# Moving the weight corrections of the first macro to VectorE and two row statistics to ScalarE

## The chip, the core and the metric

The kernel runs on one core of a Trainium2 chip. The metric is the time on the device in microseconds (us), median over several executions. Five engines run side by side, each in its own order: TensorE (PE, with its weight loads as PEld), VectorE (DVE), ScalarE (ACT), GpSimd (POOL) and SyncE (SP), which here only issues DMAs. POOL issues the gathers. Everything is float32.

## The reference

The input x has 4096 rows of 1024 numbers. Cut to what matters:

```python
xn = layernorm(x)                                  # per row, eps 1e-5
corr = irfft(abs(rfft(xn))**2)                     # autocorrelation of a row
weights, delay = top_k(corr, 6)                    # 6 = int(log(1024))
s = sum_k softmax(weights)[k] * roll(xn, -delay[k])
def qlora(x, wq, A, B):                            # weights repeat 4 times along the input
    return x @ tile(wq, (1, 4)).T + 0.5 * x @ A.T @ B.T
g = silu(qlora(silu(qlora(xn, w1)) * qlora(xn, w3), w2))   # 1024 -> 2752 -> 1024
out = x + s * g
```

## The kernel before

**Tiles.** The rows are worked on in 8 macros of 512 rows (`NR`), each of 4 tiles `r` of 128 rows. For a macro, the object `Corr` makes the normalised rows, their folded and transposed forms (`yT`, `yU`, `cT`, `bT`) and the lags; the object `Ffn` makes the feed-forward part; `Gathers` sums the six rolled copies of each tile. The folding uses that the weights repeat: TensorE sees 256 folded inputs instead of 1024.

**Order.** Nothing is scheduled by a tool. The list of functions that `plan` returns puts work before (`pre`), within (`mid`, then `half`) and after (`end`) each of the 15 steps of a macro, and every engine runs its instructions in just that order. Steps 0 to 9 are `up`: step p works on part c = p // 2 of the hidden units, two of its four blocks j. Step 10 is the rest of the hidden units, and steps 11 to 14 are the product with w2. While macro m runs, the same steps also prepare macro m+1: `stats(r)` and `norm(r)` (mean, deviation, normalising, folding), `save(r)` (two copies to DRAM for the gathers), `turn(r)` (transposes on PE), and so on.

**One block of `up`.** PE adds four matmuls into two PSUM banks that ScalarE has seeded (`seed`, L546), for the gate and the up product. ScalarE takes Silu of the gate (L582) into z, then seeds the banks of the block two further on. VectorE multiplies z by the other bank (L584), and GpSimd adds z to the sum `zf`. PE's small matmuls `u` (L552) for the LoRA part of w2 read the four z of a part one block later. There are 5 banks for the seeded sums (`psf`), and 2 for everything else of PE (`ps`), the correlation sums `e` and `o` (L433) among them.

**The first macro** does more than the others. The seed and the LoRA terms take the place of one row of the weights, so this row, held in `w0`, has to be taken off all weights first: `lessen_part(c)` loads nothing itself, but runs two instructions for part c. L146 on VectorE corrects half k = 0 and L147 on GpSimd half k = 1, each 128x1024 (part 5: 128x384). `load_first(c)` issues the load of `w0` on SP. The corrected weights stay for all macros. Parts 0 and 1 are done ahead of the first step. Parts 2 to 5 are done at `end[1]`, `end[3]`, `end[5]` and `end[7]`. PE reads part c first at step 2c: part 2 in step 4, part 3 in step 6.

The tiles `w0_2` to `w0_5` are in the pool `p3` under the tag `s`, which has three buffers. The gathered sums `s_0_0`, `s_0_1`, `s_0_2` of the tiles are in the same three buffers after them: `s_0_0` lies where `w0_3` was. Its first instruction, on ScalarE (L513), is issued at the end of step 4, between the seeds of block gu_2_3 and the Silu of z_2_2.

Also in the first macro: `mix_weights` (four sums of halves of w2 on VectorE, L170 to L173, for a product with fewer matmuls), `power(g)` for the spectra (`squares`, with the tile `o2` on ScalarE and the sum on GpSimd), `join`, and the search for the lags of the macro's own tiles: `lags(r)` in `mid[2+r]` (`corr_r`, VectorE, and a mirrored copy of it by ScalarE, L451) and `search(r)` in `end[2+r]` (L458 to L468, the six highest values).

Names as used below: z_c_j is the z of part c, block j; gu_c_j_0 and gu_c_j_1 its two banks; corr_r, search_r, norm(r) belong to tile r; x_1_r is tile r of macro 1.

## Time and profile before

| | |
|---|---|
| Median of 3 runs | 1112.71 us (1111.41 to 1113.75) |
| The profiled execution | 1112.99 us, its span 1111.2 us |
| PE busy | 1086.4 us, 98% of the span |
| DVE busy | 781.5 us, 70% |
| ACT busy | 584.9 us, 53% |
| POOL busy | 680.3 us, 61% |
| Mean granted clock of PE | 0.994 |

A span runs from the first to the last instruction, and the small difference to the execution's time lies around it. A line of the page gives an engine's operation by its source line (L577), its tiles, its busy time, the mean of one, and the idle time before it with what ended that. "PEclk" is the share of TensorE's clock that was granted. The times of a timeline are us from the span's start. A line of a timeline holds a duration that includes what the instruction waited for after its issue, so the same operation can show 0.68 in one place and 2.83 in another.

### The profile page before, as it was taken

To read this page: it belongs to the slowest core of one execution; us is meant where nothing else is said; L and a number is where in the kernel's file an instruction comes from. 1 tells how busy PE (TensorE), PEld (TensorE's weight loads), DVE (VectorE), ACT (ScalarE), POOL (GpSimd) and SP (SyncE) were. 2 spreads that over 40 slices of the span, in tenths; PEclk is the share of its full clock that TensorE was granted. 3 is DMA by queue.
4 is the path that set the end of the run, shared out by engine and by line. 5 is a ranking of instruction groups with operands and counts; after the bars stand their busy time and mean duration, and the time that the engine had idled before them with its cause. 6 is when DMAs were issued, how large, how long until landed. Compare 5 with 4: busy or idle time off the path is not lost.

```text
span 1111.2 us, 10958 instructions
## 1 busy us (share of the span) xinstructions
PE 1086.4 (98%) x3350; PEld 467.5 (42%) x3350; DVE 781.5 (70%) x1218; ACT 584.9 (53%) x1049; POOL 680.3 (61%) x535
## 2 busy tenths in 40 slices
PE   5998999999999999999999999999999999999997
PEld 4344344443444434443344434444344443444432
DVE  6799888776677776777677767677767776664543
ACT  5646634675356653665436663376534675354531
POOL 3676866677347763667546773657735677356832
PEclk9998999999999999999999999999999999999999
DMA  9852566565365653566445664556536565253533
GB/s 368 367 214 76 195 203 218 198 209 181 97 213 198 206 168 118 193 218 193 140 153 180 207 199 133 170 195 211 183 104 199 199 208 173 84 188 119 162 99 123
DMA packets 65085, 201.70 MB, mean 182 GB/s; under 512 B 7514, under 2 KB 8026, under 8 KB 64132
## 3 DMA queue, kind: packets, MB, share of 16 engines
q0 software_dynamic: 27648, 100.68, 30.0%
q1 hardware_dynamic: 37380, 100.35, 25.0%
q8 instruction: 26, 0.43, 0.2%
q14 instruction: 31, 0.25, 0.1%
HBM read 150.61 MB, written 50.39 MB: 181 GB/s over the span
## 4 chain that ended last, share of the span: by engine, by line
PE 88%; DVE 5%; issue 3%; POOL 2%; DMA 1%; ACT 1%; SPq 0%; DVEq 0%; POOLq 0%
PE gu L577 47%; PE y L653 20%; PE gu L603 3%; PE u L552 3%; PE y L663 3%; PE t L238 2%; PE fe L386 1%; PE o L433 1%; PE e L433 1%; PE fe L389 1%; PE fo L386 1%; DMA x<-in_x 1%; PE ua L254 1%; PE fo L389 1%; PE u L560 1%
## 5 line engine op out<-in xcount | busy, mean ns | idle before, releaser
L577 PE MATMUL gu<-yT,w_sb 128*128 128x512 f32 x960 | 459.8, 600 | 1.0 <-ACT gu L546 1.0
L577 PEld LDWEIGHTS gu<-yT,w_sb 128*128 128x128 f32 x960 | 176.5, 191 | 234.6 <-issue 208.5
L494 POOL DMA_INDIRECT roll<-scr,lag x192 | 232.3, 1210 | 62.6 <-issue 29.0
L516 DVE SCALAR_TENSOR_TENSOR s<-roll,w,s 128x1024 f32<-128x1024 f32 x160 | 221.8, 1386 | 1.3 <-DMA roll<-scr,lag 0.4
L546 ACT ACTIVATE gu<-second,b_sb 128x512 f32<-128x512 f32 x320 | 208.2, 686 | 4.6 <-DVE z L584 3.5
L584 DVE TENSOR_TENSOR z<-z,gu 128x512 f32<-128x512 f32 x160 | 109.5, 684 | 111.1 <-PE gu L577 75.8
L589 POOL TENSOR_TENSOR zf<-zf,z 128x512 f32<-128x512 f32 x80 | 134.4, 1680 | 79.4 <-DVE z L584 77.9
L582 ACT ACTIVATE z<-gu 128x512 f32<-128x512 f32 x160 | 95.2, 595 | 140.0 <-PE gu L577 134.7
L577 PE MATMUL gu<-yU,w_sb 128*128 128x512 f32 x320 | 164.3, 595 | 0.0
L469 POOL TENSOR_TENSOR e<-euler,e 128x6 f32<-128x6 f32 x32 | 48.6, 1519 | 145.7 <-DVE e L468 144.4
L735 POOL TENSOR_TENSOR x<-g,x 128x512 f32<-128x512 f32 x62 | 82.3, 1336 | 66.1 <-DVE g L734 23.5
L653 PE MATMUL y<-w_sb,zf 128*128 128x512 f32 x256 | 122.1, 599 | 0.0
L577 PEld LDWEIGHTS gu<-yU,w_sb 128*128 128x128 f32 x320 | 61.0, 191 | 77.2 <-issue 67.5
L734 DVE TENSOR_TENSOR g<-s,g 128x512 f32<-128x512 f32 x64 | 52.7, 854 | 43.2 <-ACT g L733 42.4
L587 POOL TENSOR_TENSOR zf<-z,z 128x512 f32<-128x512 f32 x40 | 65.4, 1634 | 24.0 <-DVE z L584 17.6
L733 ACT ACTIVATE g<-y 128x512 f32<-128x512 f32 x64 | 35.5, 593 | 78.2 <-PE y L663 45.2
L653 PEld LDWEIGHTS y<-w_sb,zf 128*128 128x128 f32 x256 | 46.2, 190 | 59.8 <-issue 57.5
L451 ACT COPY corr<-corr 128x511 f32<-128x511 f32 x32 | 19.8, 617 | 80.6 <-DVE corr L450 80.6
L653 PE MATMUL y<-w_sb,S 128*128 128x512 f32 x128 | 61.8, 605 | 0.0
L653 PE MATMUL y<-t_sb,zf 128*128 128x512 f32 x128 | 60.4, 593 | 0.3 <-DVE zf L647 0.3
L214 DVE TENSOR_TENSOR a<-x 128x512 f32<-128x512 f32 x28 | 33.8, 1209 | 26.7 <-ACT x L207 26.7
L192 DVE BATCH_NORM_STATS2 stats<-x 128x6 f32<-128x512 f32 x64 | 40.8, 677 | 4.2 <-DMA x<-in_x 4.2
(179 smaller groups left out, 1371.4 us busy)
## 6 DMA issues: line engine op xcount, KB each, us to landing
scr<-x SPq DMA_DIRECT2D x64, 512.0 KB
x<-in_x SPq DMA_DIRECT2D x32, 512.0 KB
x<-in_x SPq DMA_DIRECT2D x64, 256.0 KB
out<-x SPq DMA_DIRECT2D x64, 256.0 KB
w_sb<-in_w13t SPq DMA_DIRECT2D x5, 1024.0 KB
second<-rows SPq DMA_DIRECT2D x14, 256.0 KB
roll<-scr,lag POOLq DMA_INDIRECT x192, 5.2
w<-in_w0t SPq DMA_DIRECT2D x5, 512.0 KB
```

The source lines that it names most:

```text
L469: nc.gpsimd.tensor_tensor(e, bass.AP(euler.tensor, euler.offset, [list(euler.ap[0]), [0, TOP]]), e, ALU.pow)
L494: nc.gpsimd.indirect_dma_start(out=g, out_offset=None, in_=st.scratch[r].rearrange("p (n o) -> (p n) o", o=1), in_offset=bass.IndirectOffs ...
L516: nc.vector.scalar_tensor_tensor(s, g, w, s, ALU.mult, ALU.add)
L546: nc.scalar.activation(acc, self.st.second[:, wi, :], AF.Copy, scale=b13_sb[:, c, q : q + 1])
L577: nc.tensor.matmul(acc, lhsT=w13_sb[:, c, 2 * j + wi, k, :], rhs=y, start=False, stop=(k == 1), skip_group_check=True,)
L582: nc.scalar.activation(z, accs[0], AF.Silu)
L584: nc.vector.tensor_tensor(z, z, accs[1], ALU.mult)
L587: nc.gpsimd.tensor_tensor(self.sum_of(c), zs[0], zs[1], ALU.add)
L589: nc.gpsimd.tensor_tensor(self.zf[c], self.zf[c], z, ALU.add)
L653: nc.tensor.matmul(acc, lhsT=lhs, rhs=rhs, start=(first and a == 0), stop=True, skip_group_check=True)
L734: nc.vector.tensor_tensor(g, s(i)[:, cols], g, ALU.mult)
L735: (nc.vector if last else nc.gpsimd).tensor_tensor(xt, g, xt, ALU.add)
```

## The change

Four edits, all of which bear on the first macro alone:

- `lessen` takes the engine of its second instruction. Parts 0 and 1 keep GpSimd; parts 2 to 5 now run both instructions on VectorE, at `end[2]`, `end[4]`, `end[6]` and `end[7]`.
- The statistics of tiles 2 and 3 of macro 1 are made by a new `stats_scalar`: a sum and two sums of squares on ScalarE, then three small instructions on GpSimd. Before, VectorE made them (L192 to L196) with two small ones on GpSimd.
- `power(3)` is put ahead of the last of the four sums of w2.
- `o2` of g = 1 and 3 in macro 0 goes to the buffer `bcs` of `p1`, where it was in `x2` of `px`.

```diff
-    def lessen(w, w0):
+    def lessen(w, w0, engine=nc.vector):
         nc.vector.scalar_tensor_tensor(w(0), w0, minus, w(0), ALU.mult, ALU.add)
-        nc.gpsimd.tensor_tensor(w(1), w(1), w0, ALU.subtract)
+        engine.tensor_tensor(w(1), w(1), w0, ALU.subtract)
...
+        def stats_scalar(self, r):
+            n, xt = f"{self.m}_{r}", self.x[r]
+            total, mean, var, rstd, shift = [
+                small.tile([P, 1], F32, tag=tag, name=f"{tag}{i}_{n}") for i, tag in enumerate(("rest", "var", "var", "rstd", "shift"))
+            ]
+            squares = small.tile([P, 2], F32, tag="mv", name=f"squares_{n}")
+            nc.scalar.activation(xt, xt, AF.Identity, accum_out=total)
+            nc.scalar.activation(mean, total, AF.Copy, scale=-1.0 / (32 * L))
+            for h in range(2):
+                left = p1.tile([P, 512], F32, tag="a", name=f"left_{n}_{h}")
+                nc.scalar.activation(
+                    left, xt[:, h * 512 : (h + 1) * 512], AF.Square, bias=mean, scale=1.0 / 32, accum_out=squares[:, h : h + 1]
+                )
+            nc.gpsimd.tensor_scalar(var, squares[:, 0:1], squares[:, 1:2], EPS, ALU.add, ALU.add)
+            nc.gpsimd.tensor_tensor(rstd, var, mhalf, ALU.pow)
+            nc.gpsimd.tensor_scalar(shift, mean, rstd, 32.0, ALU.mult, ALU.mult)
+            self.parts[r] = (shift, rstd)
...
-            o2 = (p1 if m else px).tile([P, NR], F32, tag="bcs" if m else "x2", name=f"o2_{m}_{g}")
+            where = (p1, "bcs") if m or g % 2 else (px, "x2")
+            o2 = where[0].tile([P, NR], F32, tag=where[1], name=f"o2_{m}_{g}")
...
-            mid[1].extend(mix_weights[2:])
-            mid[1].append(lambda: st.power(3))
+            mid[1].extend([mix_weights[2], lambda: st.power(3), mix_weights[3]])
...
-                end[2 * c - 3].append(lambda c=c: lessen_part(c))
+                end[(2, 4, 6, 7)[c - 2]].append(lambda c=c: lessen_part(c))
...
-                stats[r].append(lambda r=r: nxt.stats(r))
+                stats[r].append(lambda r=r: nxt.stats_scalar(r) if first and r >= 2 else nxt.stats(r))
...
-    def lessen_part(c):
+    def lessen_part(c, engine=nc.vector):
         w0 = first_times.pop(c)
         if c < FULL:
-            lessen(lambda k: w13_sb[:, c, :, k, :], w0)
+            lessen(lambda k: w13_sb[:, c, :, k, :], w0, engine)
...
-        lessen_part(0)
-        lessen_part(1)
+        lessen_part(0, nc.gpsimd)
+        lessen_part(1, nc.gpsimd)
```

## The prediction

> **What bounds the kernel now.** I read the page's busy shares first: PE is busy 98% of the span, so a change pays only where PE waits or runs slowly. Then I asked for PE's waits in the first 165 us. Over the whole span the list is the same, so all that can be won lies in the first macro:

> ```profile
> PE t L315 <- DVE b_first L290: 10.7, 2, 8.9
> PE e L433 <- DVE total L477: 1.8, 1, 1.8
> PE fo L389 <- ACT e L415: 1.2, 1, 1.2
> PE gu L577 <- ACT gu L546: 1.0, 1, 1.0
> PE u L552 <- DVE z L584: 0.6, 1, 0.6
> ```

> Columns: us in total, times, longest. The first is the program's start, which the change leaves alone. The next view cuts the span into stretches of 2 us (busy time of PE, PEld, DVE, ACT, POOL, then PE's granted clock, DMA share, GB/s):

> ```profile
> 84.00:86.00 2.00, 0.44 (x4) 0.24 (x3) 2.00 (x7) 0.00 (x0) 0.00 (x0) 1.00 0.00 0
> 86.00:88.00 2.00, 0.76 (x5) 0.60 (x5) 1.22 (x7) 1.83 (x4) 0.00 (x0) 0.81 0.00 0
> 90.00:92.00 2.00, 2.00 (x3) 0.80 (x3) 1.87 (x6) 1.52 (x4) 1.05 (x1) 0.50 0.00 0
> 94.00:96.00 2.00, 2.00 (x6) 0.96 (x5) 1.67 (x5) 0.71 (x2) 1.90 (x3) 0.98 0.79 242
> ```

> Two stalls close together (84.4 to 86.3 and 87.0 to 87.9) are followed by a clock of 0.50 from 87.3 to 94.0. PE worked from 87.9 on, so some 3.1 us are lost to the clock on top of 2.8 to the stalls. What made the stalls is in VectorE's and GpSimd's timelines:

> ```profile
> 57.88 2.83 DVE L214 TENSOR_TENSOR a<-x 128x512 f32<-128x512 f32 x1
> 69.07 0.69 DVE L214 TENSOR_TENSOR a<-x 128x512 f32<-128x512 f32 x1
> 77.74 2.30 DVE L146 SCALAR_TENSOR_TENSOR w_sb<-w,minus,w_sb 128x1024 f32<-128x1024 f32 x1
> 81.58 2.56 DVE L153 TENSOR_TENSOR yc<-a 128x256 f32<-128x256 f32 x1
> 99.43 1.28 DVE L146 SCALAR_TENSOR_TENSOR w_sb<-w,minus,w_sb 128x1024 f32<-128x1024 f32 x1
> ```

> ```profile
> 56.83 3.34 POOL L147 TENSOR_TENSOR w_sb<-w_sb,w 128x1024 f32<-128x1024 f32 x1
> 81.26 2.60 POOL L147 TENSOR_TENSOR w_sb<-w_sb,w 128x1024 f32<-128x1024 f32 x1
> ```

> L214 takes 0.69 alone and 2.83 beside L147: where both engines have an instruction with two SBUF operands, one waits until the other's has ended. L147 alone holds about 2.2 us (from 57.95, when L146 ended, to 60.17). The reader is to see that these waits made corr_2 late (86.1), and PE's matmul e with the seeds behind it.

> **The change, part by part.** The sum is made against the profiled execution's 1112.99 us (span 1111.2), 0.28 above the median.

> *Removed:* four L147 on POOL with their holds of 2.2 us; VectorE's statistics of two tiles, 1.6 each (63.97 to 65.60).

> *Added on VectorE:* four L147. The trace has none there. Bounds are 1.13 (L405, same size, start to start, alone) and 2.3 (L146 when it waited); I take 1.13, since POOL has little left that holds. L146 takes 1.19 start to start.

> *Added on ScalarE, twice:* a 1024-wide pass with a sum (1.13, and 0.22 to read it, as L207 shows), a scalar (0.20, L208), two 512-wide passes with sums (0.50 + 0.22 each), gaps: 3.1. Bounds: 2.1 (three passes alone) and 3.4 (full durations).

> *Added on POOL:* one small instruction, 0.3. POOL now waits for ScalarE's sums; behind that wait stands zf, which needs a later z in any case: 0. If it weren't so, 0.3 twice.

> *Sums of w2:* T4 (L173) steps behind bT_3, which can't start before ScalarE's o2 ends (50.55). VectorE idles 1.0 there and T4 ends at 53.0 for 51.8, but the join after it waited for POOL until 52.9 anyway: 0.1. *Buffers of o2:* PE's last reads of the tile in `bcs` ended before 21 us, 17 us earlier than o2 is written: 0; half a microsecond were a reader late. *SP:* the load of w0_5, and behind it that of x_1_3, waits for part 2: issued at 71 for 69.3. VectorE used x_1_3 at 92.8 without waiting; ScalarE wants it at 95: 0, and 2 if that slack were gone.

> Now the walk. Durations start to start, from the rows: search 2.87 (66.20 to 69.07), norm 2.6 (69.07 to 71.69), corr 0.8, z 0.6, s 1.2 on VectorE; Silu 0.5, a seed 0.62, the mirrored copy L451 0.55 on ScalarE.

> 1. norm(0) starts at 57.0, when POOL's zf ends, for 60.1. corr_0 ends at 60.9 for 64.05. But ScalarE now has the statistics of tile 2 ahead of the Silu of z_1_1: 60.95 + 0.55 + 3.1 = 64.6. That Silu ran at 64.61 before. VectorE's lead of 3 us is spent, and it idles 4 us.
> 2. z_1_1 starts at 65.2, search_0 ends at 68.7, part 2 at 71.0. PE wants its second half at 70.7: 0.3 lost.
> 3. norm(1), z_1_2 and corr_1 to 74.95 (before 73.05), copy and Silu, z_1_3 ends at 76.65. PE's u, which ended at 75.97, ends at 77.6: 1.65 lost so far.
> 4. search_1 to 79.5, norm(2) to 82.6 (0.5 for POOL's zf), corr_2 ends at 83.95 for 86.1. PE reaches e at 86.1 and finds corr_2 done, and the seeds too. The stalls of 1.84 and 0.95 and the slow clock are gone.
> 5. z_2_1 ends at 85.7, search_2 at 88.6, part 3 at 90.9. Here is a new wait: `s_0_0` lies where w0_3 was, so ScalarE's first gather instruction now waits for part 3's second half, which POOL had done at 83.9. Behind it on ScalarE stand the Silu of z_2_2 and the seeds of gu_3_0: 90.9 + 1.05 + 0.5 + 0.62 = 93.1. PE arrives at 89.95 and waits 3.1.
> 6. Second seed and oc_3 to 94.0, corr_3 to 94.8, copy 0.55, statistics of tile 3 3.1, Silu 0.5: z_2_3 ends at 99.65. PE's u for this z was due at 96.6 and ends at 100.6: another 3. Before, the transposes behind u began at 99.0. So PE, 1.4 ahead at gu_3_0, is behind: **+1.6**.
> 7. From z_2_3 on VectorE has s, search_3, z, s, weights, z, s, part 4 and norm(3) before the transposes of tile 3: 13.1, and 1.15 for one zf of POOL. PE needs 13.9 to get there: **+0.3**. Later PE waited for nothing before, and VectorE idles 1.4 and 2.0 between 115 and 120: 0.

> *Slow clock.* The waits of steps 5 and 6 can bring half clock too. Most would fall between them, where PE has 3 us to spare, so it is hidden; bounds 0 and 3.3. Taken: **+0.4**.

> [...]

> Sum: 1.6 + 0.3 + 0.4 = +2.3. From 1112.99, less the 0.28: **1115.0**.

> **Rivals.**

> *A, not slower: the statistics on ScalarE are short.* Both groups lie in the serial chain of steps 1 to 6. At the lower bound of 2.1, 2.0 of the 2.3 goes: 1113.0. Any group below 3.0 brings the sum under 0.2%. For it: passes overlap (L207 lasts 1.23 and starts the next after 1.13). Against: the reads and the scalar are in the rows.

> *B, faster: ScalarE isn't held by `s_0_0`*, because part 3 is done in time. Then z_2_2 follows part 3 at once, z_2_3 ends about 97.2, PE's u 98.15 for 99.0, without slow clock: 1112.2; together with A's 2.0, 1110.2. It decides if part 3 ends before 86. Against: it stands behind z_2_1 and search_2 in VectorE's order.

> *C, slower: the half clock isn't hidden*, or comes after step 6: 3.3 for my 0.4, 1117.9. For it: the one case in this trace cost all of its time. Against: PE waits for z_2_3 at either clock.

> *D, slower: GpSimd's `e` and gathers get between VectorE's instructions* of part 2 and norm(1), 0.94 a gather: up to 2 in step 2 and 1 in step 7: 1118. Against: at 99.43 `e` waited and L146 did not.

> **How the numbers follow.** About 0.2%, 2.2 us, is what a measurement tells from no change. The forecast, with sizes that give 1113.5 to 1116.5, gets 0.50: 0.30 slower by over 0.2%, 0.20 within. A 0.16 (within), B 0.12 (faster), C 0.12 and D 0.10 (slower). So faster 0.12, same 0.36, slower 0.52. The range leaves out most of B and the far ends of C and D: 1111.2 to 1118.6.

> **What would show it.** Right: no L214 or L153 of over 2 us at 57 and 81; no wait of PE's e there, and a clock of 1.00 from 84 to 89; ScalarE idle some 4.6 before the first `s`, released by VectorE's L147; PE's gu waiting for seeds, then u for z near 97. Wrong: if PE runs from 89 to 100 without a wait, step 5 or 6 is mistaken and B holds; if the transposes of tile 3 wait for over 1 us, step 7 was too small.

## The result, and the profile after

| | before | after |
|---|---|---|
| Median | 1111.63 us (22 runs, 1111.20 to 1113.88) | 1114.68 us (22 runs, 1114.30 to 1115.58) |
| The profiled execution | 1112.99 us, span 1111.2 us | 1114.60 us, span 1112.6 us |
| Mean granted clock of PE | 0.994 | 0.996 |

The ratio after to before is 1.0025, 95% interval 1.0019 to 1.0031: the change makes the kernel slower by 0.25%. One thing has to be known to read the numbers: nearly all executions of the kernel before lie in two groups, near 1111.3 and 1113.3 us (26 of 113 in all are above 1112.4), its profiled execution is near the upper one, and those of the kernel after lie in one group.

Lines of the changed kernel stand 20 or 21 lines further down (L577 is now L598, L552 L573, L546 L567, L584 L605, L214 L234, L207 L227). On the clock of its profile the work comes 0.53 earlier: the first `o` of tile 0 is at 57.12 where it was at 57.65 (experiment 4 shows why).

PE's waits of the kernel after (us in total, times, longest; selected lines, as in all views below):

```profile
PE t L335 <- DVE b_first L310: 10.0, 2, 9.2
PE gu L598 <- ACT gu L567: 2.8, 1, 2.8
PE u L573 <- DVE z L605: 1.8, 2, 1.6
```

The 1.8 for `e` are gone, the seeds (gu) cost 2.8 for 1.0, and `u` 1.8 for 0.6. The stretches of 2 us (busy PE, PEld, DVE, ACT, POOL, then PE's clock):

```profile
84.00:86.00 2.00, 2.00 (x12) 1.30 (x11) 1.81 (x2) 1.35 (x3) 1.04 (x1) 1.00 0.00 0
86.00:88.00 2.00, 2.00 (x7) 0.92 (x6) 1.93 (x6) 0.00 (x0) 0.41 (x2) 1.00 0.00 0
90.00:92.00 2.00, 0.00 (x0) 0.00 (x0) 0.30 (x2) 1.90 (x3) 1.81 (x2) 1.00 0.00 0
94.00:96.00 2.00, 2.00 (x4) 0.82 (x3) 0.48 (x5) 1.85 (x4) 0.00 (x0) 0.50 0.47 182
```

PE now runs through 84 to 88 and stands still from 90 to 92; half clock follows the new stall. VectorE's timeline of the kernel after (start, duration, idle before it and what ended that):

```profile
55.29 1.75 DVE L234 TENSOR_TENSOR a<-x 128x512 f32<-128x512 f32 x1
64.52 0.69 DVE L605 TENSOR_TENSOR z<-z,gu 128x512 f32<-128x512 f32 x1 [4.14 <-ACT z L603]
69.17 1.22 DVE L147 TENSOR_TENSOR w_sb<-w_sb,w 128x1024 f32<-128x1024 f32 x1
80.60 0.41 DVE L153 TENSOR_TENSOR yc<-a 128x256 f32<-128x256 f32 x1
98.22 0.69 DVE L605 TENSOR_TENSOR z<-z,gu 128x512 f32<-128x512 f32 x1 [3.68 <-ACT z L603]
```

The waits of 2.83 and 2.56 behind GpSimd's L147 have gone; the 1.75 at 55.29 is a shorter one, which ends when GpSimd's `zf` does (56.49). In the profile of the kernel before, such waits went with where the operands lie. L214, with both in SBUF, was held all 12 times it met the first `zf` of a part (L587): it took 1.32 to 1.87 for 0.69 and ended 0.54 to 0.56 after `zf`. L584, with one of two in a PSUM bank, took 0.67 to 0.69 all 39 times it met a `zf` of L589. And L214 at 79.97 took 0.68 beside the 128x6 `e` (78.92 to 81.27), so not every instruction of GpSimd with two SBUF operands held it.

In place of those waits VectorE waits twice, 4.14 and 3.68, for a Silu. Why is on ScalarE's timeline of the kernel after:

```profile
60.41 0.62 ACT L472 COPY corr<-corr 128x511 f32<-128x511 f32 x1 [2.17 <-DVE corr L471]
60.93 1.05 ACT L210 ACTIVATE x<-x 128x1024 f32<-128x1024 f32 x1
63.19 0.72 ACT L215 ACTIVATE left<-x,var 128x512 f32<-128x512 f32 x1
63.91 0.57 ACT L603 ACTIVATE z<-gu 128x512 f32<-128x512 f32 x1
90.10 1.15 ACT L534 ACTIVATE s<-roll,w 128x1024 f32<-128x1024 f32 x1 [4.75 <-DVE w_sb L147]
```

The statistics hold ScalarE from 60.93 to 63.91, and at 90.10 the first gather instruction of `s_0_0` has waited 4.75 for part 3's L147 on VectorE.

### The profile page after: what moved, and what is told of

It reads as the page before. It is cut to its first block, busy times and chain, and to the rows that moved or that the text cites. A ratio compares the mean times of both kernels' runs of the same rounds, so it can differ in the third digit from the quotient of the medians.

```text
span 1112.6 us, 10967 instructions
## 1 busy us (share of the span) xinstructions
PE 1087.1 (98%) x3350; PEld 466.5 (42%) x3350; DVE 774.9 (70%) x1214; ACT 590.2 (53%) x1063; POOL 671.5 (60%) x533
## 4 chain that ended last, share of the span: by engine, by line
PE 87%; DVE 4%; issue 3%; ACT 2%; POOL 2%; DMA 2%; SPq 0%; POOLq 0%; DVEq 0%; ACTq 0%
PE gu L598 47%; PE y L674 20%; PE u L573 3%; PE gu L624 3%; PE y L684 3%; PE t L258 2%; PE o L454 1%; PE fe L406 1%; PE fe L409 1%; PE e L454 1%; DMA x<-in_x 1%; PE fo L406 1%; PE fo L409 1%; PE ua L274 1%; PE u L581 1%
## 5 line engine op out<-in xcount | busy, mean ns | idle before, releaser
L598 PE MATMUL gu<-yT,w_sb 128*128 128x512 f32 x960 | 459.0, 599 | 2.8 <-ACT gu L567 2.8
L598 PEld LDWEIGHTS gu<-yT,w_sb 128*128 128x128 f32 x960 | 175.7, 190 | 236.3 <-issue 207.0
L567 ACT ACTIVATE gu<-second,b_sb 128x512 f32<-128x512 f32 x320 | 208.3, 686 | 5.7 <-DVE z L605 4.8
L605 DVE TENSOR_TENSOR z<-z,gu 128x512 f32<-128x512 f32 x160 | 109.4, 684 | 118.6 <-PE gu L598 75.8
L598 PE MATMUL gu<-yU,w_sb 128*128 128x512 f32 x320 | 164.3, 595 | 0.0
L598 PEld LDWEIGHTS gu<-yU,w_sb 128*128 128x128 f32 x320 | 61.0, 191 | 77.2 <-issue 67.5
L234 DVE TENSOR_TENSOR a<-x 128x512 f32<-128x512 f32 x28 | 32.6, 1166 | 26.8 <-ACT x L227 26.8
L573 PE MATMUL u<-z,a_sb 128*2 128x512 f32 (+1 forms) x320 | 44.7, 594 | 1.8 <-DVE z L605 1.8
```

The lines of the kernel that those rows point to most:

```text
L567: nc.scalar.activation(acc, self.st.second[:, wi, :], AF.Copy, scale=b13_sb[:, c, q : q + 1])
L573: nc.tensor.matmul(self.u2[32 * j : 32 * j + n, :], lhsT=a2_sb[:, at : at + n], rhs=z, start=(c == 0), stop=True, skip_group_check=True,)
L598: nc.tensor.matmul(acc, lhsT=w13_sb[:, c, 2 * j + wi, k, :], rhs=y, start=False, stop=(k == 1), skip_group_check=True,)
L605: nc.vector.tensor_tensor(z, z, accs[1], ALU.mult)
```

## The experiments

All times are medians. The kernel before ran beside each, at 1111.1 to 1111.5 us. "Kernel 1" and "kernel 3" are those of experiments 1 and 3.

**1. Statistics back on VectorE.** From the kernel after:

```diff
-                stats[r].append(lambda r=r: nxt.stats_scalar(r) if first and r >= 2 else nxt.stats(r))
+                stats[r].append(lambda r=r: nxt.stats(r))
```

> The changed kernel with the statistics of tiles 2 and 3 back on VectorE (two groups of 1.6 us there, none of 3.0 on ScalarE); all else stays. Theory (steps 1, 3 and 6: the statistics stand in ScalarE's serial chain): the Silu of z_1_1 comes right after corr_0, z_1_1 some 2.5 us earlier than in the changed kernel, PE's wait of 1.6 us for u goes, part 3 ends near 87.5 for 90.1, and PE still waits some 2.3 for the seeds of gu_3_0 since step 5 is untouched. 1110.2 to 1111.9 us, taken 1111.0. Rival A (the groups are short and cost little): 1114 or more. Rival: VectorE, which gets 3.2 us of work back, becomes late for the transposes of tile 3: a wait of PE near 113 and 1113 or more.

1110.32 us (11 runs), ratio to before 0.9994 (0.9985 to 1.0003). PE's waits of this kernel have no line for `u` any more, and the one for the seeds is still there (2.3 was expected):

```profile
PE gu L598 <- ACT gu L567: 2.8, 1, 2.8
```

Part 3 ends at 87.33, and the transposes of tile 2 start 38.1 after the first `o` for 42.8. The statistics cost 4.4 us of the change, more than the whole loss.

**2. `s_0_0` elsewhere.** From the kernel after:

```diff
-                    s = self.s[st.m, r] = p3.tile([P, L], F32, tag="x" if r == RT - 1 else "s", name=f"s_{st.m}_{r}")
+                    s = self.s[st.m, r] = p3.tile([P, L], F32, tag="x" if r == RT - 1 or (st.m, r) == (0, 0) else "s", name=f"s_{st.m}_{r}")
```

> The changed kernel with the first gather sum s_0_0 in a buffer of the x tiles (free since tile 1 was saved) and not where w0_3 was; statistics stay on ScalarE. Theory (step 5: ScalarE is held by that buffer alone): ScalarE's idle 4.75 us before the first s is gone, s runs near 85.5, PE has no wait for the seeds of gu_3_0; PE then waits some 2 us for z_2_3, which comes near 96 for 98.8. Transposes at 97.1 for 99.9: 1111.9 us, 1111 to 1115 with or without a slow clock after that wait. Rival (ScalarE is held by the roll or by the weights instead, or the moved sum collides with the loads of x): the wait of PE for the seeds stays over 2 us and the time at 1114 or more.

1112.85 us (11 runs, 1111.61 to 1113.89), ratio to before 1.0013 (1.0004 to 1.0022). ScalarE's timeline and PE's waits of this kernel:

```profile
85.75 1.14 ACT L534 ACTIVATE s<-roll,w 128x1024 f32<-128x1024 f32 x1
86.80 0.58 ACT L603 ACTIVATE z<-gu 128x512 f32<-128x512 f32 x1
```

```profile
PE u L573 <- DVE z L605: 3.9, 2, 2.4
```

`s` starts without any wait, 4.3 us earlier, and the seeds are there. So it was the buffer that held ScalarE, not the gathered roll. PE then meets z_2_3, which is late for the statistics, and waits 2.4 there: the two causes lie one behind the other, and this edit alone wins 1.8.

**3. Both.** The two edits above together.

> Both: statistics on VectorE and s_0_0 in a buffer of the x tiles; parts 2 to 5 still lessened by VectorE alone and later. Theory: PE has neither the wait for u near 76 nor that for seeds near 90, nor a slow clock; transposes of tile 2 near 93 to 94 for 99.9, 1107.5 to 1109, faster than both kernels by over 0.2%. Rival (moving the second half of each part to VectorE costs by itself, by its 4.9 us in VectorE's chain): a new wait near the transposes of tile 3 (113) takes the gain back, 1111 or more.

1108.12 us (6 runs, 1107.85 to 1108.73), ratio to before 0.9969 (0.9957 to 0.9982): faster than either kernel, with L147 on VectorE and late. From 20 to 165 us PE has one wait beside those for `ua` (1.4), `fo` (1.2) and `y` (0.4) that the kernels before and after have too (1.4, 1.2, and 0.3 or 0.4):

```profile
PE u L573 <- DVE z L605: 1.0, 1, 1.0
```

The 1.0 before z_2_3 is new, since PE comes earlier. VectorE has the last part of tile 3's norm done at 107.19, and PE wants it at 107.47: only 0.28 is to spare there.

**4. The kernel before once more**, unedited, for the two groups of its executions.

> The kernel before, unedited, for its spread: its 22 executions lie at two levels, near 1111.4 and 1113.5, and the profiled one (1112.99) is nearer the upper. Theory: half clock after the stalls of 84 to 88 comes or lasts in some executions only, so an execution at 1111.4 shows the same stalls and fewer than 3 us at a clock under 0.9 near 88 to 94, and the mean clock of executions at 1113.5 is lower by 0.002. Rival: the levels come from elsewhere (the start, the loads), and the clock in that stretch is 0.50 for over 6 us at either level.

1111.49 us (11 runs, five of them at 1112.5 to 1113.6); the profiled execution took 1111.49. PE's timeline of it:

```profile
85.57 0.68 PE L433 MATMUL e<-ti_sb,pwy 128*128 128x129 f32 x4 [1.85 <-DVE total L477]
87.20 1.98 PE L577 MATMUL gu<-yT,w_sb 128*128 128x512 f32 x4 [0.95 <-ACT gu L546]
95.41 0.66 PE L238 MATMUL t<-ident,yc 128*128 128x128 f32 x4
```

The stalls are the same, 1.85 and 0.95. The difference near 90 us is the clock. Here are both profiles in stretches of 3.41 us, cut where the trace's record of the granted clock can change. First the profile shown with the prediction:

```profile
83.83:87.25 3.42, 1.29 (x9) 0.94 (x7) 2.70 (x10) 1.08 (x3) 0.03 (x1) 1.00 0.00 0
87.25:90.66 3.41, 2.74 (x4) 1.19 (x5) 3.27 (x6) 3.41 (x7) 1.27 (x1) 0.50 0.00 0
90.66:94.07 3.41, 3.41 (x6) 1.34 (x5) 3.25 (x11) 2.52 (x6) 2.90 (x3) 0.50 0.00 0
```

And the second profile of the same kernel:

```profile
81.90:85.32 3.42, 1.82 (x8) 0.91 (x6) 3.42 (x7) 0.00 (x0) 1.24 (x1) 1.00 0.15 62
85.32:88.73 3.41, 2.21 (x8) 1.33 (x9) 2.59 (x9) 3.27 (x5) 1.27 (x1) 1.00 0.00 0
88.73:92.14 3.41, 3.41 (x10) 1.50 (x9) 3.21 (x11) 2.52 (x6) 1.72 (x2) 1.00 0.00 0
```

In the first, 2.13 us of the stalls fall into one stretch, and the next two run at 0.50. In the second they are split, 1.60 and 1.20, and the clock stays. The transposes of tile 2 start 41.35 after the first `o` in the first and 38.47 in the second. Of the 2.88, 1.42 are lost again up to the next `fe` (25.12 for 23.70 from the transposes), part of it where PE waits for VectorE's `yc` of tile 3. At the end of the span 0.8 is left: the spans are 1111.2 and 1109.7, and of these 1.5 us the other 0.7 lies before the first `o` (57.65 and 56.94). There the first profile has one more stretch at half clock, which the second has not:

```profile
18.98:22.39 3.41, 3.41 (x19) 3.41 (x18) 3.03 (x6) 2.79 (x10) 0.00 (x0) 0.50 1.03 418
```

The profiles of experiments 3 and 5 have such a stretch as well, and their first `o` is at 57.84 and 57.70; in the eleven profiles without one it lies between 56.94 and 57.19.

Do the two profiles stand for the two groups? Of the 91 executions with a mean clock on record, the 19 above 1112.4 us show 0.994 or 0.995, and 68 of the 72 others 0.996 or more (the other four, at 1112.0 to 1112.3, show 0.995). So the groups go with the clock. That the slow stretch is near 90 us in every execution of the upper group is not shown; the medians of the groups lie 2.0 apart, the two profiled executions 1.5.

**5. Parts early, on VectorE.** From kernel 1:

```diff
-                end[(2, 4, 6, 7)[c - 2]].append(lambda c=c: lessen_part(c))
+                end[2 * c - 3].append(lambda c=c: lessen_part(c))
```

> The changed kernel with statistics on VectorE and parts 2 to 5 lessened by VectorE at the places of the kernel before (in steps 1, 3, 5, 7 in place of 2, 4, 6, 7); s_0_0 stays where w0_3 was. Theory: lateness is the fault of step 5, not VectorE. Part 3 is then done near 77.5, before s_0_0 is wanted, so PE has no wait for seeds near 90; norm(0) starts 1.3 us later for part 2, which later steps absorb: 1107.7 to 1109 us, like the kernel with both undone (1108.1). Rival (VectorE's own 2.4 us in front of norm(0) make z_1_1 and all behind it late): a wait of PE for u near 73 of over 1 us and 1109.5 or more.

1108.43 us (6 runs: four at 1108.2 to 1108.5, two at 1110.0 and 1110.4), ratio to before 0.9971 (0.9958 to 0.9983). The seeds no longer wait for part 3. The details differ from the expectation: L146 of part 3 waited for GpSimd's `zf` (2.31), part 3 ended at 80.36, and PE waited 0.84 for `e` and 0.95 for seeds near 84 to 86. Those two put 1.79 idle into one stretch, and half clock followed in the profiled execution, which is the one at 1110.4.

**6. GpSimd's L147 at the new places.** From kernel 3:

```diff
-    def lessen_part(c, engine=nc.vector):
+    def lessen_part(c, engine=nc.gpsimd):
```

> The kernel with both undone (1108.1), but the second half of parts 2 to 5 on GpSimd again, at the new, later places. Theory (the hold of 2.2 us is the price of GpSimd's L147, 1.22 that of VectorE's): norm(1) and z_2_2 start about 1.0 us later each than with VectorE alone, PE waits 0.5 more for part 2 near 68 and some 2 to 3 us for z_2_3 near 92: 1109.2 to 1111.5, taken 1110.2. Rival (moving the second half to VectorE is worth nothing, since what follows waits for GpSimd's zf or for PE anyway): 1107.8 to 1108.5.

1111.94 us (11 runs, 1110.53 to 1113.29), ratio to before 1.0003 (0.9994 to 1.0012): 3.8 us slower than kernel 3, more than expected, and for another reason. PE's waits and GpSimd's timeline:

```profile
PE gu L598 <- POOL w_sb L147: 2.6, 2, 2.4
```

```profile
87.13 2.30 POOL L490 TENSOR_TENSOR e<-euler,e 128x6 f32<-128x6 f32 x1 [1.59 <-DVE e L489]
89.41 2.34 POOL L147 TENSOR_TENSOR w_sb<-w_sb,w 128x1024 f32<-128x1024 f32 x1
```

L147 stands behind `e` in GpSimd's order, so part 3 itself is done at 91.75, and PE waits for the weights, not for VectorE. On VectorE (kernel 3) it was done at 88.2. Half clock followed the wait in the profiled execution; the two executions with the highest mean clock (0.998) took 1110.53 and 1110.63, 2.5 above kernel 3.

**7. Sums of w2 and buffers of o2 as before.** From kernel 3:

```diff
-            mid[1].extend([mix_weights[2], lambda: st.power(3), mix_weights[3]])
+            mid[1].extend(mix_weights[2:])
+            mid[1].append(lambda: st.power(3))
...
-            where = (p1, "bcs") if m or g % 2 else (px, "x2")
-            o2 = where[0].tile([P, NR], F32, tag=where[1], name=f"o2_{m}_{g}")
+            o2 = (p1 if m else px).tile([P, NR], F32, tag="bcs" if m else "x2", name=f"o2_{m}_{g}")
```

> The kernel with both undone (1108.1), but the fourth sum of w2 and the buffers of o2 as in the kernel before. Theory (this part was priced at 0.1): 1107.8 to 1108.4. Rival (the two edits free VectorE or ScalarE for half a microsecond or hold them for one): the time moves by 0.4 or more to either side.

1108.04 us (5 runs, 1107.02 to 1108.70) for 1108.12: no difference that these runs can tell.

**8. The statistics alone, in the kernel before** (`stats_scalar` added there, and):

```diff
-                stats[r].append(lambda r=r: nxt.stats(r))
+                stats[r].append(lambda r=r: nxt.stats_scalar(r) if first and r >= 2 else nxt.stats(r))
```

> The kernel before with only the statistics of tiles 2 and 3 moved to ScalarE. Theory (steps 1 and 6): the Silu of z_1_1 runs 3.0 us later (67.6 for 64.6), z_1_1 and what follows on VectorE 2.4 later, PE waits some 3 us for u near 74 for 0.6, and again for z_2_3: 1114 to 1117 us, taken 1115.5. Rival A (the groups are short and VectorE gains 3.2 us): 1111.5 or less.

1115.69 us (5 runs), ratio to before 1.0035 (1.0022 to 1.0049): 4.4 us above the 1111.3 beside it, as much as in experiment 1 from the other side. The size was right, the place not quite. PE's waits of this kernel:

```profile
PE gu L597 <- ACT gu L566: 3.2, 2, 2.2
PE u L572 <- DVE z L604: 2.0, 2, 1.2
PE e L453 <- DVE total L497: 1.9, 1, 1.9
```

PE lost 2.2 near 66 to 68 for seeds that stood behind the statistics on ScalarE, not 3 for `u` near 74 (0.7 there).

**9, 10. One tile's statistics at a time.** From the kernel after, tile 2 back on VectorE, then (for the other run) tile 3:

```diff
-                stats[r].append(lambda r=r: nxt.stats_scalar(r) if first and r >= 2 else nxt.stats(r))
+                stats[r].append(lambda r=r: nxt.stats_scalar(r) if first and r == 3 else nxt.stats(r))
...
-                stats[r].append(lambda r=r: nxt.stats_scalar(r) if first and r >= 2 else nxt.stats(r))
+                stats[r].append(lambda r=r: nxt.stats_scalar(r) if first and r == 2 else nxt.stats(r))
```

> The changed kernel with the statistics of tile 2 alone back on VectorE; those of tile 3 stay on ScalarE. Theory (step 1): up to the seeds of gu_3_0 all runs as with both tiles on VectorE, 2.7 us ahead of the changed kernel. Then tile 3's statistics (3.0 us on ScalarE) make z_2_3 end near 96.1, PE waits about 1.5 for it and starts the transposes near 97.1 for 99.9: 1112.3 us, 1111.8 to 1114. Rival (the statistics cost only where they come second, step 6): 1114 or more.

> The changed kernel with the statistics of tile 3 alone back on VectorE; those of tile 2 stay on ScalarE. Theory (step 6, and that the half clock of the changed kernel is hidden behind PE's wait for z_2_3): PE starts gu_3_0 at 92.4 as in the changed kernel, z_2_3 ends near 96.8, so PE no longer waits for it. Executions in which no half clock follows the wait of 2.8 start the transposes near 98.1 for 99.9, 1112.9 us; those with a half clock of 3.4 us lose 1.7 of it again, 1114.6 us: two levels. Rival (the half clock isn't what the levels come from): one level near 1113. Rival (step 6 is mistaken): 1114.7 throughout.

1111.92 and 1112.77 us (11 runs each), ratios to before 1.0008 (0.9999 to 1.0017) and 1.0012 (1.0003 to 1.0021). Each tile's statistics cost by themselves: 2.8 for tile 2, 1.9 for tile 3 (0.9 by experiment 11). With tile 2 on VectorE the transposes start at 97.22 (97.1 expected), though PE's wait for z_2_3 is 0.26 and not 1.5, since half clock fills the rest. With tile 3 on VectorE two levels were expected and these executions showed one, at 1112.6 to 1113.4. The profiled one kept its clock, with PE's wait of 3.36 split over two stretches:

```profile
87.94:91.36 3.42, 1.68 (x4) 0.38 (x2) 2.71 (x5) 0.64 (x1) 2.73 (x2) 1.00 0.00 0
91.36:94.77 3.41, 1.78 (x4) 0.87 (x5) 1.58 (x5) 2.52 (x6) 1.85 (x2) 1.00 0.51 153
94.77:98.18 3.41, 3.41 (x13) 0.76 (x11) 3.28 (x8) 3.41 (x7) 1.21 (x2) 1.00 0.00 1
```

**11. The tile 3 kernel once more**, unedited.

> The kernel with tile 3's statistics alone on VectorE, unedited, for one more profile: its executions lay at one level (1112.6 to 1113.4) where two had been expected. If half clock comes by the idle share of stretches of 3.41 us on a grid that is free against the program, this profile's grid lies elsewhere: over some 1.8 us of PE's wait of 3.4 near 91 in one stretch is followed by 3.41 us at 0.50, PE starts the transposes near 100.0 for 98.4 and the execution takes 1114 or more. If the clock stays at 1.00 with over 2.2 idle in one stretch, that reading is wrong.

1113.77 us (8 runs: four at 1112.9 to 1113.5, four at 1114.1 to 1114.4). The profiled execution took 1114.17:

```profile
88.19:91.60 3.41, 1.38 (x4) 0.31 (x2) 1.89 (x2) 1.49 (x2) 3.22 (x2) 1.00 0.00 0
91.60:95.01 3.41, 2.63 (x3) 1.18 (x4) 2.36 (x8) 2.52 (x6) 2.13 (x2) 0.50 0.46 144
95.01:98.43 3.42, 3.42 (x5) 1.35 (x4) 3.35 (x7) 3.12 (x6) 2.06 (x3) 0.50 0.03 10
```

2.03 us idle in one stretch, then half clock, and transposes at 99.97 for 98.41. The two levels are there after all. Why the eleven executions of the first time all kept to one is not known.

**12. The kernel after once more**, unedited.

> The changed kernel, unedited, for one more profile. Prediction's term for the slow clock: half clock between the waits of steps 5 and 6 is hidden, since PE waits for z_2_3 at either clock. The transposes start 42.8 us after the first o of tile 0, as in the first profile, with half clock near 94 or without; without it PE's wait for u near 97 is some 1.9 for 0.24. The time is 1114.3 to 1115.2 either way. Rival C (half clock isn't hidden): an execution without it is shorter by 1 us or more.

1114.78 us (8 runs, 1114.25 to 1115.11). The transposes start 42.81 after the first `o` (42.80 in the first profile), again with one stretch at half clock (93.50 to 96.91) and a wait of 0.23 for z_2_3. Neither profile of this kernel is without that stretch, so that half clock is hidden rests on its one level of times, and on PE having to wait for z_2_3 even at half clock. The record of the clock fits: of its 30 executions the three with the highest mean clock (0.998) took 1114.27, 1114.34 and 1115.11, where all lie between 1114.25 and 1115.58.

## Why the prediction was right

Read as a ladder, the change is one gain and two losses that are together twice as large:

| | us | step |
|---|---|---|
| kernel before | 1111.4 | |
| L147 of parts 2 to 5 on VectorE, old places, with the edits to w2 and o2 (5) | 1108.43 | -3.0 |
| parts at the new, later places (1) | 1110.32 | +1.9 |
| statistics of two tiles on ScalarE (after) | 1114.68 | +4.4 |

The first gain is as large as the whole loss that was measured (3.05). The other two take it back twice: the later places through the buffer of `s_0_0` (with `s_0_0` elsewhere they cost nothing, 1108.12 in experiment 3), and the statistics through ScalarE's order.

By the prediction's steps, with 0.53 added to the times of after:

1. *Step 1.* corr_0 ended at 60.91 (60.9 predicted); the group of statistics took 2.98 (3.1); z_1_1 started at 65.05 (65.2). VectorE idled 4.14 (4).
2. *Step 2.* L147 took 1.15 start to start (1.13); PE lost 0.38 (0.3).
3. *Step 3.* `u` ended at 77.74 (77.6); experiment 9 shows that tile 2's statistics were the cause.
4. *Step 4.* corr_2 ended at 83.54 (83.95), since norm(2) met no wait for `zf`. The stalls and the slow clock there are gone, as said. What the step took for granted was wrong: that the slow clock is in every execution of the kernel before.
5. *Step 5.* Part 3 ended at 90.6 (90.9), ScalarE idled 4.75 (4.6), PE waited 2.80 (3.1). Experiment 2 shows that the buffer does it.
6. *Step 6.* z_2_3 ended at 99.36 (99.65), `u` at 100.45 (100.6): +1.45 for the predicted +1.6.
7. *Step 7.* PE took the transposes of tile 3 without a wait: 0 for +0.3. The chain was 0.3 shorter than the time PE needs.

The term for the *slow clock*, +0.4, measured 0: half clock came and filled the wait for z_2_3, which was the reason given. So against the profile it was worked out from, the sum should have been +1.45, and the two profiled executions differ by 1.61 (1114.60 less 1112.99). Not all of this is the chain of steps 1 to 7: the start gave 0.53, and some 0.4 were lost at the matmuls `ua` near 118 (6.73 from `u` to `fe` for 6.32). No run looked into the latter; the second profile of the kernel before takes 7.11 there, so it isn't the change alone.

The medians differ by 3.05, because the base was high. Steps 4 to 6 credited the change with 2.8 us of stalls and 3.1 of slow clock. The stalls are in both profiles of the kernel before, the slow clock in one alone, and by the mean clocks most executions lack it: for them that credit is not there to be had. This is the step that failed. Its size was wrong too: without the slow clock the transposes of tile 2 came 2.88 earlier, but the end only 0.8. With the 0.7 of the start, these 0.8 are what the profiled execution lay above the second one. That the time still came out within 0.3 us is luck: the first median, 1112.71, was 1.1 above the 1111.63 measured with the result (and 1.3 above the 1111.4 of all 113 executions), and the predicted difference of 2.3, with two terms that were too large (0.3 and 0.4), was 0.75 below the 3.05 measured. The mechanism of steps 1 to 6 is no luck: experiments 1, 2, 3 and 9 take it apart.

*Rival A* (the groups are short) fell: 2.98 each. Its point of decision was wrong as well: groups just below 3.0 were to bring the loss under 0.2%, and it is 0.25%. *Rival B* (ScalarE isn't held) fell by 4.75 us of idle time. *Rival C* (half clock not hidden) fell for this kernel; experiment 11 shows what it costs where nothing hides it, 1.6 us at the transposes. *Rival D* (GpSimd's `e` and gathers between VectorE's instructions) was not seen in steps 2 and 7; in the first profile with tile 3 on VectorE, one instruction of search_1 (L483) took 0.80 for 0.23, to 79.57, where GpSimd's `zf` ended at 79.53, and part 3 came 0.6 later. It looks like a wait of the same kind, for another instruction of GpSimd; this one time is all that shows it.

## What to carry to other kernels

Before moving a buffer's last use later, look up which tile comes into that buffer next and what stands behind its first write: here a late use on one engine held another engine's seeds and cost 1.9 us, and a free buffer cost nothing. Before moving work to an engine that is idle half the time, look whether it will stand in the chain that sets the end: ScalarE was 53% busy, and 3 us put ahead of a Silu cost 1 to 3 us a time. And before a stretch at half clock is credited to a change, profile the kernel before a second time.

## What the hardware showed that was not expected

GpSimd's L147 cost 3.8 us against VectorE's (experiments 3 and 6), though the rows differ by 1.1 (2.34 and 1.22): its place behind `e` in GpSimd's order made PE wait 2.4 for the weights, and in the profiled execution half clock followed that wait (90.84 to 97.66).
